# The Mamba gate turned round: D x and the gate applied with the inner dimension on partitions, and three VectorE duties moved to ScalarE and GpSimd

## The chip, the cores and the metric

The kernel runs on one core of one Trainium2 chip. A core has TensorE (PE; its weight loads are listed as PEld), VectorE (DVE), ScalarE (ACT), GpSimd (POOL) and SyncE (SP, which here only issues DMAs). Each engine takes its own instructions in the order in which the program lists them, and waits for the others through semaphores. The metric is the device time of one launch in microseconds (us); less is better.

## The reference, cut to what matters

x is 4 x 512 x 1024 (batch, time, channels), all in float32. The block is a Mamba mixer with adaptive layer norm, followed by a second mixer over four streams. The change concerns the first half alone:

```
h = layernorm(x) * (1 + ca) + sa                 # ca, sa: modulations of the batch row
x, z = split(h @ in_proj_w)                      # each 2048 inner channels ("d")
xc = silu(conv_b + sum_k conv_w[:, k] * x shifted by 3-k)   # 4 taps along time
dt_r, B, C = rmsnorm of the parts of xc @ x_proj_w.T        # 64, 16, 16 columns
dt = softplus(dt_r @ dt_proj_w.T + dt_bias)
per channel d and state n (16 of them), along time:
    state = exp(dt * A[d, n]) * state + dt * B[n] * xc
    ys   += C[n] * state
y = (ys + D * xc) * silu(z)
out = x + ga * (y @ out_proj_w.T)
```

The second half takes a layer norm of that, 24 logits a row, 50 Sinkhorn iterations on 4 x 4 matrices, and mixes four streams of 256 channels.

## The kernel before, in words

**Tiling.** Time is cut into 8 blocks of 256 (`TB`; two blocks make a batch row), `k` in the code. A block's 2048 inner channels are 16 chunks of 128 partitions, four chunks a quad (`q`, 4 quads a block, 32 in all, numbered `m`). So a tile `xc`, `u`, `dv` or `w` holds 128 partitions (channels) x 4 chunks x 256 times, 128x1024 in the profile.

**The scan loop.** The heart is 512 steps: 8 blocks x 4 quads x 16 states. For one state of one quad GpSimd makes `w = u * B` (`emit_w`, L917, two steps ahead), ScalarE makes `da = exp(dt * A)` into PSUM (`emit_exp`, L933, one step ahead), VectorE runs four scans along time in place in `w` (L963), TensorE transposes `w` so that time comes onto the partitions (`emit_turn`, L943, 8 transposes of 128x128 into `hq`, in the next step), and VectorE adds `hq * C` to `acc` (`emit_sum`, L952, two instructions of 128x512, in the next step: C is then one number a partition). `w` has three buffers, `hq` two, `da` two.

**What is put between.** `step` calls `tick` six times. A tick lets one VectorE filler out of `gaps` (a convolution tap, a norm's statistics: whatever yielded "v"), wakes the tasks whose time has come (`due`; a task yields how many ticks it sleeps: `LAG` 2, `TAP_LAG` 3, `ACT_LAG` 5, `POOL_LAG` 10), and lets `paced` issue some matmuls of the product queue. The queue (`products`) holds for block `k`: the x products of block k+1 and the output products of block k-1, alternating, then one z product, then more of both, `product_bc`, and z products. `paced` spreads these over the ticks by their columns plus an allowance `ASIDE` for work on the side; when the product at the head cannot go on (it yields 0: no bank, or an input not yet issued), nothing of the queue is issued until it can, and the columns owed are then made up at up to 1.3 times the rate. The main loop runs under a manual schedule: the order in which these calls are made is the order on each engine.

**Around the change.** `product_x` (L423) makes x of a chunk in a PSUM bank; ScalarE takes tap 3 and the bias out of it into `xc` (L448), VectorE adds taps 0 to 2 (L455), and after the fourth chunk ScalarE makes the sigmoid from tanh in a scratch tile `sg` (tag `tmp`, two buffers; L464, L465) and GpSimd multiplies (L467). `product_z` (L473) makes z with time on the partitions (`ht` is the stationary operand) and forms silu(z) in `sz`. `stage_dt` (L586), called in step 3 of the quad before, makes `dt` by softplus (L608, with a table load before and after it on ScalarE), `u = dt * xc` (L616), and then D x: ScalarE scales `xc` by D into scratch `xd` (L621), TensorE transposes it (L633), ScalarE copies it to `acc` (L638), which is where the 16 sums start from. `gate_quad` (L730), spawned in step 2 of the next quad, multiplies `acc` by `sz` on GpSimd (L735), transposes the product back (L749) and copies it to `y` (L756), the input of `product_out` (L656). `front` (L773) does the second layer norm and the logits of the block before.

**Buffers.** `xc` has five, freed by `stage_dt`; `row` tiles (128x1024) five; `sz` and `acc` two each.

## Time and profile before

| What | Value |
|---|---|
| median of 3 runs | 2709.85 us (2709.05 to 2709.86) |
| the profiled execution | 2702.3 us, span 2700.5 us, granted TensorE clock 0.94 |
| the scan loop in it | 154.6 to 2415.3 us, 512 steps |
| blocks of the loop, 1st to 8th | 315.8, 277.3, 278.7, 280.5, 279.3, 281.1, 276.1, 272.6 us |
| VectorE busy in the loop | 2090.8 of 2260.7 us |
| GpSimd busy in the loop | 1659.0 us |
| ScalarE busy in the loop | 1549.9 us |

The profile is one execution recorded by the hardware. Busy times are those of the instructions themselves; an instruction's listed duration overlaps the start of the next a little, so what one costs in a row of them is the distance between starts. In a group's row stand line, engine, operation, output <- inputs, shapes and count, then the summed time and the mean in ns, then the engine's idle time just before these instructions and what ended most of it. "x2048" of a float32 matmul counts two records for each matmul of the program; a transpose is one record. Steps are counted by the scans: a step runs from its first scan to the next step's.

### The profile page before, as it was taken

To read this page: it belongs to the slowest core of one execution; us is meant where nothing else is said; L and a number is where in the kernel's file an instruction comes from. 1 tells how busy PE (TensorE), PEld (TensorE's weight loads), DVE (VectorE), ACT (ScalarE), POOL (GpSimd) and SP (SyncE) were. 2 spreads that over 40 slices of the span, in tenths; PEclk is the share of its full clock that TensorE was granted. 3 is DMA by queue.
4 is the path that set the end of the run, shared out by engine and by line. 5 is a ranking of instruction groups with operands and counts; after the bars stand their busy time and mean duration, and the time that the engine had idled before them with its cause. 6 is when DMAs were issued, how large, how long until landed. Compare 5 with 4: busy or idle time off the path is not lost. (4 is left out here: it accounts for less than half of the span.)

```text
span 2700.5 us, 39703 instructions
## 1 busy us (share of the span) xinstructions
PE 2408.1 (89%) x13392; PEld 2051.6 (76%) x13392; DVE 2361.0 (87%) x4451; ACT 1716.9 (64%) x3755; POOL 1731.8 (64%) x1167
## 2 busy tenths in 40 slices
PE   8999989999999989998999899998999899885446
PEld 8887478888788878887888788887888777675435
DVE  0349898999999999999999999999999899977898
ACT  0356567666776777667776776668666856633445
POOL 0146557777976688768766786779676977931014
PEclk9979989999999999999999999999999899896769
DMA  5432523333433343234333433333333323225302
GB/s 184 152 125 94 204 75 130 113 106 121 154 117 104 116 153 121 106 114 149 125 110 114 156 118 109 118 145 125 121 106 124 130 94 117 83 74 203 153 31 110
DMA packets 74347, 331.06 MB, mean 123 GB/s; under 512 B 8496, under 2 KB 25312, under 8 KB 47456
## 3 DMA queue, kind: packets, MB, share of 16 engines
q1 hardware_dynamic: 62784, 311.56, 32.1%
q10 hardware_dynamic: 11360, 16.96, 1.7%
q8 instruction: 107, 1.75, 0.3%
q14 instruction: 96, 0.79, 0.1%
HBM read 303.14 MB, written 25.35 MB: 122 GB/s over the span
## 5 line engine op out<-in xcount | busy, mean ns | idle before, releaser
L917 POOL TENSOR_TENSOR w<-u,b 128x1024 f32<-128x1024 f32 x512 | 1209.1, 2363 | 558.2 <-PE hq L943 413.5
L933 ACT ACTIVATE da<-dv,aneg 128x256 f32<-128x256 f32 x2048 | 971.5, 477 | 616.5 <-DVE w L963 571.5
L963 DVE TENSOR_TENSOR_SCAN w<-da,w 128x256 f32<-128x256 f32 x2048 | 1263.3, 667 | 69.5 <-ACT da L933 47.6
L952 DVE SCALAR_TENSOR_TENSOR acc<-hq,ss,acc 128x512 f32<-128x512 f32 x1024 | 724.6, 735 | 78.2 <-PE hq L943 73.1
L943 PE MATMUL hq<-ident,w 128*128 128x128 f32 x4096 | 644.1, 282 | 73.1 <-DVE acc L952 53.7
L943 PEld LDWEIGHTS hq<-ident,w 128*128 128x128 f32 x4096 | 511.8, 146 | 220.7 <-issue 57.7
L487 PE MATMUL pz<-w_z,ht 128*128 128x256 f32 x2048 | 517.2, 387 | 0.0
L439 PE MATMUL pp<-ht,w_x 128*128 128x259 f32 x2048 | 511.5, 387 | 0.0
L667 PE MATMUL po<-y,w_out 128*128 128x256 f32 x2048 | 496.2, 381 | 5.4 <-ACT dv L608 5.4
L439 PEld LDWEIGHTS pp<-ht,w_x 128*128 128x128 f32 x2048 | 372.1, 193 | 46.2 <-issue 0.4
L667 PEld LDWEIGHTS po<-y,w_out 128*128 128x128 f32 x2048 | 368.6, 191 | 46.5 <-ACT dv L608 6.9
L487 PEld LDWEIGHTS pz<-w_z,ht 128*128 128x128 f32 x2048 | 369.2, 195 | 36.5 <-issue 0.3
L455 DVE SCALAR_TENSOR_TENSOR xc<-pp,cw,xc 128x256 f32<-128x256 f32 x384 | 178.4, 464 | 31.8 <-ACT xc L448 30.7
L1212 POOL TENSOR_TENSOR o<-o,x 128x1024 f32<-128x1024 f32 x16 | 37.7, 2354 | 189.1 <-ACT dg L1158 142.2
L1197 PE MATMUL oa<-h,dg 128*128 128x256 f32 x256 | 62.8, 389 | 74.9 <-ACT dg L1158 69.5
L1197 PEld LDWEIGHTS oa<-h,dg 128*128 128x128 f32 x256 | 49.3, 195 | 84.1 <-ACT dg L1158 76.5
L467 POOL TENSOR_TENSOR xc<-xc,sx 128x1024 f32<-128x1024 f32 x32 | 75.5, 2358 | 42.8 <-ACT sx L465 42.8
L448 ACT ACTIVATE xc<-pp,cb,cw 128x256 f32<-128x256 f32 x128 | 71.3, 557 | 47.5 <-PE pp L439 47.4
L749 PE MATMUL py<-ident,acc 128*128 128x128 f32 x256 | 48.4, 324 | 54.7 <-ACT dv L608 28.3
L262 PEld LDWEIGHTS pm<-sc,w_mod 128*128 128x128 f32 x384 | 80.9, 323 | 9.0 <-DVE mv_a L358 9.0
L262 PE MATMUL pm<-sc,w_mod 128*128 128x4 f32 x384 | 79.5, 343 | 9.1 <-DMA w_mod<-wmod_dram 9.1
L749 PEld LDWEIGHTS py<-ident,acc 128*128 128x128 f32 x256 | 34.8, 167 | 67.2 <-ACT dv L608 25.2
(172 smaller groups left out, 2303.2 us busy)
## 6 DMA issues: line engine op xcount, KB each, us to landing
w_x<-in_w_dram SPq DMA_DIRECT2D x64, 1024.0 KB, 4.7
w_z<-in_w_dram SPq DMA_DIRECT2D x64, 1024.0 KB, 4.9
w_out<-out_w_dram SPq DMA_DIRECT2D x56, 1024.0 KB, 4.8
w_mod<-wmod_dram SPq DMA_DIRECT2D x24, 1024.0 KB, 4.8
b<-bcd SPq DMA_DIRECT2D x32, 512.0 KB, 3.8
xt<-x_dram SPq DMA_DIRECT2D x16, 512.0 KB, 8.2
xr<-x_dram SPq DMA_DIRECT2D x32, 256.0 KB, 5.1
x<-xr ACTq DMA_DIRECT2D x32, 256.0 KB, 2.5
```

The source lines that it names most:

```text
L262: pe.matmul(pm[:, 2 * q + j, :], w[:, k, j * P : (j + 1) * P], sc[:, k, :], start=(k == 0), stop=(k == HC - 1),)
L439: pe.matmul(pp, w[:, h, j * P : (j + 1) * P], hts[k][:, h, :], start=(h == 0), stop=(h == HC - 1),)
L455: vec.scalar_tensor_tensor(xc[:, c, :], pp[:, tap : tap + TB], cw[:, i, tap : tap + 1], xc[:, c, :], ALU.mult, ALU.add,)
L487: pe.matmul(pz[:, t, :], hts[k][:, h, PAD + t * P : PAD + (t + 1) * P], w[:, h, :], start=(h == 0), stop=(h == HC - 1),)
L667: pe.matmul(po, w[:, d - lo, :], ys[k, d // QC][:, d % QC, :], start=(d == lo), stop=(d == hi - 1),)
L749: pe.transpose(py[:, j, t * P : (t + 1) * P], acc[:, t, c * P : (c + 1) * P], ident)
L917: pool.tensor_tensor(w, us[k, q], bts[k, n // NG][:, n % NG, :].unsqueeze(1).to_broadcast([P, QC, TB]), ALU.mult,)
L933: act.activation(da[:, j, :], dts[k, q][:, 2 * s + j, :], AF.Exp, scale=aneg[:, i, n : n + 1])
L943: pe.transpose(h[:, c * P : (c + 1) * P], ws[g][:, c, t * P : (t + 1) * P], ident)
L952: vec.scalar_tensor_tensor(acc[:, t, :], hqs.pop((g, t)), cts[k][:, t, n : n + 1], acc[:, t, :], ALU.mult, ALU.add,)
L963: vec.tensor_tensor_scan(w[:, c, :], das[g, c // 2][:, c % 2, :], w[:, c, :], 0.0, ALU.mult, ALU.add)
L1197: pe.matmul(oa[:, n, :], dg[:, n, m, :], hs[m] if m < NS else ybs[i], start=(m == 0), stop=(m == NS),)
```

## The change

Seven things are edited together.

- `product_z` swaps the operands: the weights are stationary and z comes out with channels on the partitions. `sz` has the layout of `xc`.
- `gate_quad` no longer multiplies ahead of the transposes. It transposes `acc` (now the sum over states alone), copies it to `y`, has ScalarE scale `xc` by D into a scratch tile, has GpSimd add it to `y`, and ten ticks later multiply `y` by `sz`.
- `stage_dt` therefore loses the D x scaling, its 8 transposes and the two copies.
- The first state's sum (`n == 0`) is a scaled copy on ScalarE from `hq` to `acc`, since `acc` has no starting value any more.
- `product_x` lets ScalarE scale a second tap (tap 2) into a scratch tile `sx`, taken when the quad's first x product begins; VectorE adds two taps in place of three; GpSimd adds `sx` to `xc`, and ten ticks later the sigmoid begins in `sx`.
- `xc` tiles live until the gate has read them ("xd" in place of "dt" as the mark), with six buffers in place of five; `row` tiles have four in place of five. A `sz` tile is free when `y` is done, not when the transposes are issued.
- `ASIDE` goes down by 2048, the columns of a block's 32 transposes.

```diff
@@ -111,7 +111,7 @@
 
 
 
-        free = {"mm": 4, "tmp": 2, "row": 5, "xr": 2, "ao": 2, "sgz": 1}
+        free = {"mm": 4, "tmp": 2, "row": 4, "xr": 2, "ao": 2, "sgz": 1}
         done = set()
         gaps = deque()
         waiting = deque()
...
@@ -427,10 +428,12 @@
             w = weights.pop(("x", k, p))
             m = NQ * k + q
             if p % 2 == 0:
-                if m >= 5:
-                    yield from until(("dt", m - 5), 0)
-                xcs[k, q] = quad_tile(f"xc_{k}_{q}", "xc", 5)
-            xc = xcs[k, q]
+                if m >= 6:
+                    yield from until(("xd", m - 6), 0)
+                xcs[k, q] = quad_tile(f"xc_{k}_{q}", "xc", 6)
+                yield from take("tmp", 0)
+                sxs[k, q] = scratch(f"sx_{k}_{q}")
+            xc, sx = xcs[k, q], sxs[k, q]
             for j in range(2):
                 i = 2 * p + j
                 yield from take("mm", 0)
...
@@ -449,8 +452,12 @@
                         xc[:, c, :], pp[:, PAD:], AF.Identity,
                         bias=cb[:, i : i + 1], scale=cw[:, i, KC - 1 : KC],
                     )
+                    act.activation(
+                        sx[:, c, :], pp[:, PAD - 1 : PAD - 1 + TB], AF.Copy,
+                        scale=cw[:, i, KC - 2 : KC - 1],
+                    )
                     yield TAP_LAG
-                    for tap in range(KC - 1):
+                    for tap in range(KC - 2):
                         yield "v"
                         vec.scalar_tensor_tensor(
                             xc[:, c, :], pp[:, tap : tap + TB], cw[:, i, tap : tap + 1],
...
@@ -459,12 +466,12 @@
                     give("mm")
                     if c == QC - 1:
                         yield LAG
-                        yield from take("tmp")
-                        sg = scratch(f"sx_{k}_{q}")
-                        act.activation(sg, xc, AF.Tanh, scale=0.5)
-                        act.activation(sg, sg, AF.Copy, scale=0.5, bias=0.5)
+                        pool.tensor_tensor(xc, xc, sx, ALU.add)
+                        yield POOL_LAG
+                        act.activation(sx, xc, AF.Tanh, scale=0.5)
+                        act.activation(sx, sx, AF.Copy, scale=0.5, bias=0.5)
                         yield ACT_LAG
-                        pool.tensor_tensor(xc, xc, sg, ALU.mult)
+                        pool.tensor_tensor(xc, xc, sx, ALU.mult)
                         give("tmp")
                         done.add(("xc", k, q))
 
...
@@ -476,16 +483,16 @@
                 yield from until(("h", k), 0)
                 m = NQ * k + q
                 if m >= 2:
-                    yield from until(("gate", m - 2), 0)
-                szs[k, q] = p1.tile([P, TT, 2, 2 * P], F32, name=f"sz_{k}_{q}", tag="sz", bufs=2)
-            sz = szs[k, q]
+                    yield from until(("y",) + divmod(m - 2, NQ), 0)
+                szs[k, q] = quad_tile(f"sz_{k}_{q}", "sz", 2)
+            sz = szs[k, q][:, 2 * s : 2 * s + 2, :]
             yield from take("mm", 0)
             w = weights.pop(("z", k, q, s))
-            pz = bank(f"pz_{k}_{q}_{s}", (P, TT, 2 * P))
-            for t in range(TT):
+            pz = bank(f"pz_{k}_{q}_{s}", (P, 2, TB))
+            for j in range(2):
                 for h in range(HC):
                     pe.matmul(
-                        pz[:, t, :], hts[k][:, h, PAD + t * P : PAD + (t + 1) * P], w[:, h, :],
+                        pz[:, j, :], w[:, h, j * P : (j + 1) * P], hts[k][:, h, PAD:],
                         start=(h == 0), stop=(h == HC - 1),
                     )
                     yield TB
...
@@ -495,13 +502,13 @@
             def finish():
                 yield LAG
                 yield from take("sgz")
-                sg = p1.tile([P, TT, 2 * P], F32, name=f"sgz_{k}_{q}_{s}", tag="sgz")
+                sg = p1.tile([P, 2, TB], F32, name=f"sgz_{k}_{q}_{s}", tag="sgz")
                 act.activation(sg, pz, AF.Tanh, scale=0.5)
-                act.copy(sz[:, :, s, :], pz)
+                act.copy(sz, pz)
                 give("mm")
                 act.activation(sg, sg, AF.Copy, scale=0.5, bias=0.5)
                 yield ACT_LAG
-                pool.tensor_tensor(sz[:, :, s, :], sz[:, :, s, :], sg, ALU.mult)
+                pool.tensor_tensor(sz, sz, sg, ALU.mult)
                 give("sgz")
                 if s == 1:
                     done.add(("sz", k, q))
...
@@ -614,30 +621,7 @@
             u = quad_tile(f"u_{k}_{q}", "u", 2)
             us[k, q] = u
             pool.tensor_tensor(u, dv, xc, ALU.mult)
-            yield from take("tmp")
-            xd = scratch(f"xd_{k}_{q}")
-            for c in range(QC):
-                i = QC * q + c
-                act.activation(xd[:, c, :], xc[:, c, :], AF.Copy, scale=dpar[:, i : i + 1])
-                if c % 2:
-                    yield LAG
             yield LAG
-            if NQ * k + q >= 2:
-                yield from until(("gate", NQ * k + q - 2))
-            acc = p1.tile([P, TT, QC * P], F32, name=f"acc_{k}_{q}", tag="acc", bufs=2)
-            accs[k, q] = acc
-            for t in range(TT):
-                yield from take("mm")
-                pa = bank(f"pa_{k}_{q}_{t}", (P, QC * P))
-                for c in range(QC):
-                    pe.transpose(
-                        pa[:, c * P : (c + 1) * P], xd[:, c, t * P : (t + 1) * P], ident
-                    )
-                aside(QC * TURN)
-                yield LAG
-                act.copy(acc[:, t, :], pa)
-                give("mm")
-            give("tmp")
             if k % NH:
 
                 e0 = p2.tile([P, N, QC], F32, name=f"e0_{k}_{q}", tag="e0")
...
@@ -731,11 +715,6 @@
 
             m = NQ * k + q
             acc = accs[k, q]
-            yield from until(("sz", k, q))
-            pool.tensor_tensor(
-                acc, acc, szs[k, q].rearrange("p t s c -> p t (s c)"), ALU.mult
-            )
-            yield POOL_LAG
             if m >= 6:
                 yield from until(("out", (m - 6) // NQ))
             y = quad_tile(f"y_{k}_{q}", "y", 6)
...
@@ -755,6 +734,20 @@
                 yield LAG
                 act.copy(y[:, 2 * s : 2 * s + 2, :], py)
                 give("mm")
+            yield from take("tmp")
+            xd = scratch(f"xd_{k}_{q}")
+            for c in range(QC):
+                i = QC * q + c
+                act.activation(xd[:, c, :], xcs[k, q][:, c, :], AF.Copy, scale=dpar[:, i : i + 1])
+                if c % 2:
+                    yield LAG
+            done.add(("xd", m))
+            yield LAG
+            pool.tensor_tensor(y, y, xd, ALU.add)
+            give("tmp")
+            yield POOL_LAG
+            yield from until(("sz", k, q))
+            pool.tensor_tensor(y, y, szs[k, q], ALU.mult)
             done.add(("y", k, q))
 
 
...
@@ -856,7 +849,7 @@
         XC, ZC, OC = 2 * HC * TB, 4 * HC * TB, DC * TB
         BC = 2 * DC * P
         SPLIT = DC - QC
-        ASIDE = 12416
+        ASIDE = 10368
 
         def products(k):
 
...
@@ -948,6 +941,17 @@
 
             if g >= 0:
                 k, q, n = where(g)
+                if n == 0:
+                    m = NQ * k + q
+                    if t == 0:
+                        assert m < 2 or ("gate", m - 2) in done
+                        accs[k, q] = p1.tile(
+                            [P, TT, QC * P], F32, name=f"acc_{k}_{q}", tag="acc", bufs=2
+                        )
+                    act.activation(
+                        accs[k, q][:, t, :], hqs.pop((g, t)), AF.Copy, scale=cts[k][:, t, 0:1]
+                    )
+                    return
                 acc = accs[k, q]
                 vec.scalar_tensor_tensor(
                     acc[:, t, :], hqs.pop((g, t)), cts[k][:, t, n : n + 1], acc[:, t, :],
...
```

The same two buffer counts (`row` 4, `xc` 6) also stand where such tiles are made for the modulation rows and the partial output products.

More of the change, by code (lines that the diff above doesn't have):

```diff
@@ L229, in row_tile @@
         def row_tile(name):
-            return p1.tile([P, H], F32, name=name, tag="row", bufs=5)
+            return p1.tile([P, H], F32, name=name, tag="row", bufs=4)
         def bank(name, shape):
@@ L301, in finish @@
                 yield from take("row")
-                mr = p1.tile([B, 3, TB], F32, name=f"mr_{kind}_{q}", tag="row", bufs=5)
+                mr = p1.tile([B, 3, TB], F32, name=f"mr_{kind}_{q}", tag="row", bufs=4)
                 m, sg, ab = mr[:, 0, :], mr[:, 1, :], mr[:, 2, :]
@@ L341, in load_constants @@
             vec.tensor_scalar(aneg, aneg, -1.0, None, ALU.mult)
-        hts, xcs, bts, cts, ets, szs, dts, us, accs, ys, aos, parts, e0s = ({} for _ in range(13))
+        hts, xcs, sxs, bts, cts, ets, szs, dts = ({} for _ in range(8))
+        us, accs, ys, aos, parts, e0s = ({} for _ in range(6))
         def normalize(xts, name):
@@ L681, in finish_part @@
                 if i % QC == 0:
-                    parts[i // QC] = quad_tile(f"part_{i // QC}", "xc", 5)
+                    parts[i // QC] = quad_tile(f"part_{i // QC}", "xc", 6)
                 act.activation(parts[i // QC][:, i % QC, :], po, AF.Copy, scale=scale)
```

## The prediction

> **What bounds the kernel now.** I read the page's busy shares first, then stretches of the scan loop (154.6 to 2415.3 us, 512 steps in eight blocks of 64), then the groups by line, then the order of time inside single steps. One middle block (columns: PE, PEld, DVE, ACT, POOL busy, granted clock, DMA share, GB/s):
>
> ```profile
> PE 2408.1 (89%) x13392; PEld 2051.6 (76%) x13392; DVE 2361.0 (87%) x4451; ACT 1716.9 (64%) x3755; POOL 1731.8 (64%) x1167
> ```
>
> ```profile
> 1026.40:1306.90 280.50, 264.48 (x1528) 227.91 (x1527) 263.19 (x455) 194.91 (x395) 218.45 (x177) 0.98 0.34 124
> ```
>
> VectorE works 263 of 280 us and bounds the block, but TensorE shows 264. VectorE's 17 idle us are the room for "faster for free"; TensorE's and GpSimd's limits lie close behind. The groups that the change touches:
>
> ```profile
> L963 DVE TENSOR_TENSOR_SCAN w<-da,w 128x256 f32<-128x256 f32 x2048 | 1263.3, 667 | 69.5 <-ACT da L933 47.6 <-POOL w L917 15.0 <-POOL w L922 5.1
> L952 DVE SCALAR_TENSOR_TENSOR acc<-hq,ss,acc 128x512 f32<-128x512 f32 x1024 | 724.6, 735 | 78.2 <-PE hq L943 73.1
> ...
> L455 DVE SCALAR_TENSOR_TENSOR xc<-pp,cw,xc 128x256 f32<-128x256 f32 x384 | 178.4, 464 | 31.8 <-ACT xc L448 30.7
> ...
> L735 POOL TENSOR_TENSOR acc<-acc,sz 128x1024 f32<-128x1024 f32 x32 | 75.5, 2359 | 13.2 <-DVE acc L952 13.1
> ...
> L621 ACT ACTIVATE xd<-xc,dpar 128x256 f32<-128x256 f32 x128 | 57.3, 495 | 0.0
> ...
> L700 ACT ACTIVATE ao<-po,mod_t 128x256 f32<-128x256 f32 x56 | 25.6, 458 | 1.6 <-PE po L667 1.6
> ```
>
> Means overlap with the next instruction, so I price by spacing of starts. In the order of time, VectorE's and TensorE's instructions beside each other (start, us, what):
>
> ```profile
> 1000.42 2.42 DVE L963 TENSOR_TENSOR_SCAN w<-da,w 128x256 f32<-128x256 f32 x4
> 1002.76 1.47 DVE L952 SCALAR_TENSOR_TENSOR acc<-hq,ss,acc 128x512 f32<-128x512 f32 x2
> 1004.14 2.42 DVE L963 TENSOR_TENSOR_SCAN w<-da,w 128x256 f32<-128x256 f32 x4
> ```
>
> ```profile
> 1003.71 1.03 PE L487 MATMUL pz<-w_z,ht 128*128 128x256 f32 x4
> 1004.58 0.60 PE L400 MATMUL pt<-ident,xt 128*128 128x128 f32 x4
> 1005.01 0.60 PE L487 MATMUL pz<-w_z,ht 128*128 128x256 f32 x2
> ```
>
> Four scans take 2.34 (1000.42 to 1002.76). A step of scans and sums alone, 3.64 us where nothing waits, leaves 1.30 for two sums; a tap fills 0.39 (822.66 to 823.05). Four records of 256 columns take 0.87 (1003.71 to 1004.58), and a program matmul is two of them: 0.433; four transposes take 0.43 (1004.58 to 1005.01). So a step has 0.87 us of transposes plus, at the usual six to seven matmuls, some 3.9 us of TensorE against 3.64 to 4.8 of VectorE.
>
> The reader should also see what happens where TensorE's work comes in a bunch. Near the loop's end the output products stand in six steps:
>
> ```profile
> 2375.08 2.42 DVE L963 TENSOR_TENSOR_SCAN w<-da,w 128x256 f32<-128x256 f32 x4
> 2380.05 0.75 DVE L952 SCALAR_TENSOR_TENSOR acc<-hq,ss,acc 128x512 f32<-128x512 f32 x1 [2.55 <-PE hq L943]
> ...
> 2387.87 0.24 DVE L829 SCALAR_TENSOR_TENSOR lg<-plg,r,base 128x24 f32<-128x24 f32 x1 [3.43 <-PE plg L820]
> ```
>
> The sum cannot start, because its transposes stand behind the bunch on TensorE.
>
> **The change, part by part.** Counts are from the instruction order of both built programs.
>
> VectorE loses 64 sums (1024 to 960) and 128 taps (384 to 256). In the loop that is 64 x 0.65 = 41.6 and, since the first block's 16 taps come before the loop, 112 x 0.39 = 43.7: together -85.3 us if nothing takes their place.
>
> TensorE loses 256 transposes of D x (256 x 0.108 = 27.7 us). The gate product is turned round at the same count and 387 ns a record: nothing.
>
> ScalarE gains 128 reads of a tap from PSUM. None exists; the nearest row is L700 (458 ns, scaled, from PSUM), the ends L621 (495) and L448 (557); spaced, 0.46: 59 us. The first state's scaled read takes the place of the copy of D x (585 ns, same shape): nothing. The D x scaling only moves, from after the softplus to directly ahead of it.
>
> GpSimd gains 64 additions of 128x1024 (2.36 us, the price of L735): +151 us. Its load in this block goes from 218 to some 235 of 280, so on average it fits. SP's queue has the same number of rows, and no DMA is added; a weight lands in 4.7 us and is loaded three products ahead, so its moves cost nothing unless a whole product's lead (3.5 us or more) is lost. One row buffer fewer: 0 to 8.2 us (an xt landing) a block; I take 0, since a front's rows are not needed before the next block's bunch.
>
> The new waits are in the order. The old gate multiplied first and then transposed; now a quad's output exists only after transposes, copy, D x, addition and multiplication. Behind it stand the last block's output products on TensorE. And xc exists only after an extra GpSimd addition with ten ticks' delay: behind it stands the B/C product. Third, the sixth quad's buffer is freed by the D x read and needs a scratch buffer that is now held through the whole convolution: behind it stand the x products. The planner leaves TensorE nearly empty there and pays the debt back at once. A step of an engine runs from its first instruction for that step (TensorE: the step's first transposes) to the next one's, and its load is counts times the spacings above. From the order, in us: steps 1 to 4 of the fourth block now hold 1.30, 2.17, 1.73, 0.87 of TensorE work, steps 5 to 9 hold 5.20, 6.96, 8.00, 6.06, 5.67, where VectorE has 3.64, 3.64, 3.64, 5.01, 4.03. Before, the bunch was 5.20 and 6.10 in two steps. There are two more now: steps 35 and 36 (6.12, 5.66) and 45 and 46 (6.51, 6.14).
>
> To price a bunch I carry a lag: each step adds TensorE's work less VectorE's, never below zero. What exceeds 1.30 + 2.34 - 0.87 = 2.8 us (sums and scans during which the transposes may still come) is a VectorE wait. Test: in the last 16 steps of before this gives 12.9 us; VectorE idled 14.0 there. ScalarE likewise: the exponentials of a half must come within two scans and two sums less their own length, 1.17 + 1.30 - 0.92 = 1.55. At a softplus ScalarE now has, in steps 18 and 19, 4.74 + 8.42 us (before 3.84 + 6.97), because D x and the copies stand there too. When one wait is paid, the other lag shrinks by as much.
>
> Over the loop the rule gives 102 us of waits before (TensorE 39, ScalarE 64) and 222 after (107 and 115): +119; by block before 27, 9, 11, 10, 11, 10, 9, 18 and after 32, 22, 28, 27, 28, 27, 30, 29. With wider allowances (4.2 and 2.8) it gives 61 and 159: +98. I take the middle, +108. The rule is short of the truth: VectorE idled 170 us in the loop of before, some 38 of them in the start of the first block.
>
> Outside the loop: B/C of the first block waits for the last xc (TensorE waited 6.3 us for it), which is one addition later: +2.4. At the end, the old 2.43 us multiplication before the transposes goes, and four D x (1.8) and two operations (4.7) follow the copy: +4.1, all on the path.
>
> Sum: -85.3 + 108 + 2.4 + 4.1 = +29. The profiled execution took 2702.3 us (span 2700.5), so 2732; it lies 7.5 us under the median of the runs shown, 2709.85, and on that scale the forecast is 2740.
>
> A rule that disagrees: the Trainium skill, "Perfetto Trace Analysis", section "Identifying the Most-Contended Engine", says to judge TensorE's headroom by its weight-load busy share and to relieve the busiest engine first. By that row, 228 of 280 us, TensorE has a fifth to spare and its bunches would cost nothing, which is the first rival's time. The waits of 2.55 and 3.43 us above speak against an average of either kind.
>
> **The rivals.** First, TensorE's bunches are free: ScalarE's waits of the same steps cover them, or the lag spreads. Then the 68 us of added TensorE waits go from +119: -85.3 + 51 + 6.5 = -28, 2682 on the median's scale. For it: GpSimd and ScalarE delays near step 3 give TensorE time. Against: the 14.0 us measured at the loop's end. It decides as soon as TensorE's added waits are below some 40 us.
>
> Second, the rule under-counts the new waits as it does the old ones (170 against 102, times 1.66), with GpSimd's queue as the third engine: two additions and two multiplications fall into single steps (7.56 us in step 5), and the next w, which scan and transposes need, stands behind them. 108 x 1.66 = 179: +101, 2811. Against: much of the missing 68 us is the loop's start.
>
> Third, gain and waits cancel within 0.2% (what a measurement tells from no change, 5.4 us): waits of 73 to 84 us. Nothing favours that exactly.
>
> That the change does not do what it says is excluded by the counts.
>
> **How the numbers follow.** Forecast 0.52, first rival 0.20, second 0.20, third 0.08. The forecast's own ends are its two allowances, +19 and +40: 2729 to 2750. The range reaches below the first rival and most of the way to the second: 2678 to 2798. Slower is forecast and second rival, 0.72; faster 0.20; same 0.08.
>
> **What would show it.** Right: VectorE's busy time in the loop 85 us lower; its waits for the transposes well over 100 us against 73; waits in steps 6 to 10 of blocks 2 to 7; a middle block of 280 to 288 us. Wrong: a middle block under 275, waits for transposes unchanged (first rival), or waits of the scans for GpSimd's w far above 15 us (second).

## The result, and the profile after

The changed kernel takes 2755.16 us (median of 4 runs, 2753.11 to 2763.7) against 2709.85: 1.0171 times the time before, with a 95% interval of 1.0155 to 1.0187. The ratio makes it 46.3 us slower; the two medians alone differ by 45.3. Its profiled execution took 2763.7 us (span 2761.9), the slowest of the four, and the profiled execution of before lay 7.5 us under its median, so a comparison of the two traces shows 61 us: the start is 2.3 us longer (the first scan at 156.9 against 154.6), the loop 61.5 us (156.9 to 2479.9, the end of the last scan; before 154.6 to 2416.0, since the 2415.3 given above is the start of its last scan), and the end 2.5 us shorter.

First the page's line of busy times, then a middle block in the view by stretches (length, then busy time of PE, PEld, DVE, ACT and POOL, granted clock, DMA share, GB/s), then the groups that the change touches.

```profile
PE 2427.7 (88%) x13136; PEld 2051.0 (74%) x13136; DVE 2286.5 (83%) x4259; ACT 1763.9 (64%) x3883; POOL 1875.7 (68%) x1231
```

```profile
1044.30:1330.40 286.10, 263.71 (x1493) 225.02 (x1491) 252.60 (x430) 200.65 (x410) 235.74 (x185) 0.98 0.34 121
```

```profile
L967 DVE TENSOR_TENSOR_SCAN w<-da,w 128x256 f32<-128x256 f32 x2048 | 1257.2, 668 | 122.8 <-ACT da L926 91.7
...
L956 DVE SCALAR_TENSOR_TENSOR acc<-hq,ss,acc 128x512 f32<-128x512 f32 x960 | 679.7, 736 | 159.7 <-PE hq L936 156.3
L936 PE MATMUL hq<-ident,w 128*128 128x128 f32 x4096 | 660.0, 289 | 168.7 <-DVE acc L956 115.5
...
L651 PE MATMUL po<-y,w_out 128*128 128x256 f32 x2048 | 505.4, 388 | 22.3 <-POOL y L750 22.3
...
L462 DVE SCALAR_TENSOR_TENSOR xc<-pp,cw,xc 128x256 f32<-128x256 f32 x256 | 119.3, 466 | 46.5 <-ACT sx L455 45.8
```

VectorE did lose its work: 252.60 us in this block against 263.19. The block became 5.6 us longer all the same, because VectorE now idles 33.5 us in it and idled 17.3. In the groups, its waits for the transposes rose from 73.1 to 156.3 us, those of the scans for `da` from 47.6 to 91.7. Over the loop VectorE is busy 70.9 us less and idle 132.4 us more.

Where in a block? This table is worked out from the starts of the scans in the traces: us taken by groups of four steps, mean of blocks 2 to 7. The last column is the mean block.

| steps | 0-3 | 4-7 | 8-11 | 12-15 | 16-19 | 20-23 | 32-35 | 36-39 | 44-47 | block |
|---|---|---|---|---|---|---|---|---|---|---|
| before | 17.8 | 19.4 | 16.8 | 16.9 | 17.4 | 18.2 | 17.3 | 18.2 | 17.5 | 278.8 |
| after | 17.3 | 21.4 | 23.9 | 15.4 | 17.3 | 19.3 | 16.7 | 20.6 | 18.8 | 285.9 |

Many groups gain a little; the loss is 7.1 us in steps 8 to 11, 2.0 in steps 4 to 7, 2.4 in steps 36 to 39, 1.3 in steps 44 to 47. Counted step by step in the same blocks, VectorE's idle time in steps 6 to 10, where the prediction looked for the new waits, rose from 1.9 to 10.0 us a block. The first three groups of the fifth block after, by stretches (columns as above):

```profile
1330.44:1348.41 17.97, 13.90 (x60) 10.02 (x58) 15.11 (x28) 15.36 (x37) 13.41 (x8) 0.75 0.29 110
1348.41:1369.77 21.36, 16.50 (x89) 13.88 (x89) 14.86 (x26) 13.20 (x30) 19.27 (x11) 0.97 0.21 75
1369.77:1394.37 24.60, 24.60 (x152) 22.03 (x151) 18.59 (x34) 14.16 (x31) 13.03 (x8) 1.00 0.38 129
```

TensorE gets 60 instructions in the first four steps (110 before), then 152 in steps 8 to 11 (97 before), and there it is busy without a gap while VectorE works 18.59 of 24.60 us. The order of time shows how it comes to that, first TensorE, then VectorE (start, us, what, and in brackets the idle time ahead with what ended it):

```profile
1352.68 4.48 PE L651 MATMUL po<-y,w_out 128*128 128x256 f32 x20
...
1358.30 0.60 PE L936 MATMUL hq<-ident,w 128*128 128x128 f32 x4
1361.81 1.13 PE L651 MATMUL po<-y,w_out 128*128 128x256 f32 x4 [2.90 <-POOL y L750]
...
1367.14 0.60 PE L936 MATMUL hq<-ident,w 128*128 128x128 f32 x4
```

```profile
1360.82 2.42 DVE L967 TENSOR_TENSOR_SCAN w<-da,w 128x256 f32<-128x256 f32 x4
1367.78 0.75 DVE L956 SCALAR_TENSOR_TENSOR acc<-hq,ss,acc 128x512 f32<-128x512 f32 x1 [4.54 <-PE hq L936]
```

TensorE waits 2.90 us for the last multiplication that makes `y`, then works off output and x products, and the next transposes of a state stand behind them until 1367.14. VectorE has finished its scans at 1363.24 and stands still for 4.54 us.

### The profile page after: what moved, and what is told of

Its sections match the earlier page's. It is cut to its first block, busy times and chain, and to the rows that moved or that the text cites. A ratio compares the mean times of both kernels' runs of the same rounds, so it can differ in the third digit from the quotient of the medians.

```text
span 2761.9 us, 39302 instructions
## 1 busy us (share of the span) xinstructions
PE 2427.7 (88%) x13136; PEld 2051.0 (74%) x13136; DVE 2286.5 (83%) x4259; ACT 1763.9 (64%) x3883; POOL 1875.7 (68%) x1231
## 5 line engine op out<-in xcount | busy, mean ns | idle before, releaser
L967 DVE TENSOR_TENSOR_SCAN w<-da,w 128x256 f32<-128x256 f32 x2048 | 1257.2, 668 | 122.8 <-ACT da L926 91.7
L956 DVE SCALAR_TENSOR_TENSOR acc<-hq,ss,acc 128x512 f32<-128x512 f32 x960 | 679.7, 736 | 159.7 <-PE hq L936 156.3
L936 PE MATMUL hq<-ident,w 128*128 128x128 f32 x4096 | 660.0, 289 | 168.7 <-DVE acc L956 115.5
L651 PE MATMUL po<-y,w_out 128*128 128x256 f32 x2048 | 505.4, 388 | 22.3 <-POOL y L750 22.3
L494 PE MATMUL pz<-ht,w_z 128*128 128x256 f32 x2048 | 508.7, 386 | 0.0
L442 PE MATMUL pp<-ht,w_x 128*128 128x259 f32 x2048 | 501.5, 385 | 0.0
L651 PEld LDWEIGHTS po<-y,w_out 128*128 128x128 f32 x2048 | 379.1, 195 | 67.7 <-POOL y L750 24.3
L494 PEld LDWEIGHTS pz<-ht,w_z 128*128 128x128 f32 x2048 | 371.1, 194 | 41.7 <-issue 1.3
L462 DVE SCALAR_TENSOR_TENSOR xc<-pp,cw,xc 128x256 f32<-128x256 f32 x256 | 119.3, 466 | 46.5 <-ACT sx L455 45.8
L604 PE MATMUL pd<-et,dtw 64*128 64x256 f32 x256 | 88.0, 475 | 6.3 <-ACT et L577 4.5
L451 ACT ACTIVATE xc<-pp,cb,cw 128x256 f32<-128x256 f32 x128 | 70.9, 554 | 35.1 <-PE pp L442 35.1
L469 POOL TENSOR_TENSOR xc<-xc,sx 128x1024 f32<-128x1024 f32 x32 | 75.5, 2359 | 25.9 <-DVE xc L462 25.9
L511 POOL TENSOR_TENSOR sz<-sz,sgz 128x512 f32<-128x512 f32 x64 | 81.6, 1275 | 6.1 <-ACT sgz L509 5.7
```

Of the source, the lines that this page charges most:

```text
L442: pe.matmul(pp, w[:, h, j * P : (j + 1) * P], hts[k][:, h, :], start=(h == 0), stop=(h == HC - 1),)
L462: vec.scalar_tensor_tensor(xc[:, c, :], pp[:, tap : tap + TB], cw[:, i, tap : tap + 1], xc[:, c, :], ALU.mult, ALU.add,)
L494: pe.matmul(pz[:, j, :], w[:, h, j * P : (j + 1) * P], hts[k][:, h, PAD:], start=(h == 0), stop=(h == HC - 1),)
L604: pe.matmul(pd[:, j, :], dtw[:, (QC * q + c) * P : (QC * q + c + 1) * P], ets[k][:R, :], start=True, stop=True,)
L651: pe.matmul(po, w[:, d - lo, :], ys[k, d // QC][:, d % QC, :], start=(d == lo), stop=(d == hi - 1),)
L936: pe.transpose(h[:, c * P : (c + 1) * P], ws[g][:, c, t * P : (t + 1) * P], ident)
```

## The experiments

The theory to test: the loss is one of order. `y` is issued later, the product queue finds its head not ready, and TensorE's work comes in a bunch in front of the transposes. The rivals: the 151 us of additions on GpSimd cost time of themselves; ScalarE's added or moved work does; or the first state's sum is worse off on ScalarE. The table gives every kernel that ran as a ratio to the kernel before on the same chip. "Against before" is that ratio in us of 2709.85, and differences between kernels below are differences in this column, so that runs on different chips can be set beside each other.

| kernel | median us | ratio (95% interval) | against before, us |
|---|---|---|---|
| after | 2755.16 | 1.0171 (1.0155 to 1.0187) | +46.3 |
| e1: after, queue's head changed | 2713.76 | 1.0020 (1.0011 to 1.0030) | +5.4 |
| e2: before, `y` marked ten ticks late | 2745.28 | 1.0135 (1.0119 to 1.0150) | +36.6 |
| e3: gate part alone | 2786.83 | 1.0288 (1.0260 to 1.0317) | +78.0 |
| e4: convolution part alone | 2683.41 | 0.9908 (0.9893 to 0.9923) | -24.9 |
| e5: after without GpSimd's additions | 2712.16 | 1.0018 (1.0007 to 1.0029) | +4.9 |
| e6: after without ScalarE's D scaling | 2748.97 | 1.0150 (1.0125 to 1.0176) | +40.6 |
| e7: e4, queue's head, shorter delay | 2661.79 | 0.9825 (0.9811 to 0.9840) | -47.4 |
| e8: e1 without the gate's delay | 2716.58 | 1.0027 (1.0017 to 1.0036) | +7.3 |
| e9: after, additions behind the chain | 2775.63 | 1.0234 (1.0209 to 1.0259) | +63.4 |
| e10: after, first sum on VectorE | 2738.96 | 1.0106 (1.0084 to 1.0128) | +28.7 |
| e11: e8 with a shorter delay before tanh | 2747.98 | 1.0142 (1.0121 to 1.0164) | +38.5 |
| e12: before, queue's head changed | 2684.97 | 0.9904 (0.9888 to 0.9921) | -26.0 |

### e1: another head of the product queue

The queue of a block begins with two x products instead of one, so an output product that waits for `y` comes later. Every instruction stays; only their order changes.

```diff
+                add_x(k + 1, 0, 1)
                 for i in range(4):
-                    add_x(k + 1, i, i + 1)
+                    if i < 3:
+                        add_x(k + 1, i + 1, i + 2)
                     if k:
```

> The changed kernel with one reordering of its product queue: a block begins with two x products, and each output product of the block before comes one x product later. No instruction is added or removed. Theory (the change's waits come from products that find their input not yet issued, so that TensorE stands empty and then works in a bunch): the empty steps 1 to 4 of a block hold 4.37, 4.36, 2.61, 0.87 us of TensorE work in place of 1.30, 2.17, 1.73, 0.87 and steps 7 and 8 3.94 and 4.94 in place of 8.00 and 6.06; the lag rule takes off 32 us, so about 2723 us, with VectorE's waits for the transposes some 44 us under the changed kernel's 156. Rival (the added work of ScalarE and GpSimd is what costs, wherever TensorE's work stands): as the changed kernel, 2755 us within 6.

Measured: 40.9 us less than after. The same twelve steps of the fifth block, by stretches, and VectorE's two waits:

```profile
1308.33:1325.38 17.05, 17.03 (x94) 13.76 (x93) 15.80 (x30) 13.80 (x35) 14.31 (x8) 1.00 0.35 136
1325.38:1346.51 21.13, 17.68 (x92) 15.12 (x91) 15.72 (x27) 15.99 (x32) 21.05 (x12) 0.92 0.36 125
1346.51:1363.71 17.20, 17.20 (x116) 15.64 (x115) 16.66 (x30) 12.90 (x32) 13.39 (x8) 1.00 0.26 93
```

```profile
DVE acc L958 <- PE hq L938: 100.7, 98, 8.0
DVE w L969 <- ACT da L928: 98.1, 62, 5.3
```

TensorE has 94 instructions in the first four steps, and steps 8 to 11 take 17.20 us instead of 24.60. The waits for the transposes fall from 156.3 to 100.7 us, those for `da` do not (98.1 against 91.7). The bunch costs time, and it comes from the order. Steps 4 to 7 stay at 21.13 us: GpSimd is busy there for 21.05 of them, but that this is what holds them was not tested in this order.

### e2: only the delay, in the kernel before

```diff
                 give("mm")
+            yield 10
             done.add(("y", k, q))
```

> The kernel before, with one line more: a quad's output y is marked as there 10 ticks (1.7 steps) later. No instruction is added, removed or changed; only the queue's products that ask for y are issued later. Theory: the same empty steps and bunch as in the changed kernel, at the start of each block and at the loop's end; the lag rule adds 30 us, so 2740 us, and the waits for the transposes rise from 73 to some 105 us. Rival (added work costs, not the order): 2710 us, no change.

Measured: +36.6 us. By stretches, steps 4 to 7 and 8 to 11 of its fifth block, and the wait:

```profile
1345.18:1366.53 21.35, 16.14 (x78) 13.42 (x76) 15.04 (x25) 15.80 (x35) 9.94 (x5) 0.76 0.02 3
1366.53:1389.02 22.49, 22.49 (x123) 19.74 (x122) 18.19 (x32) 11.89 (x26) 12.14 (x6) 1.00 0.42 154
```

```profile
DVE acc L953 <- PE hq L944: 117.6, 130, 8.2
```

No instruction was added to or taken from an engine, and the picture of after appears: an emptier TensorE, then 22.49 us of 22.49. Together with e1 this shows the forecast's mechanism from both sides.

### e12: the same head in the kernel before

The edit of e1, made in the kernel before.

> The kernel before with the reordered queue head alone. Theory: the bunch of steps 4 and 5 (5.20 and 6.10 us) is shared out; the rule takes off 9 us: 2700 us, 2692 to 2706. It tells how much of the best kernel's 48 us is the order and how much the convolution's part. Rival (the old order cost nothing): 2709 us within 3.

Measured: -26.0 us, more than the 10 expected. So e1's 40.9 us cannot all be put down to the change; the queue's order was worth 26.0 without it. But it acts elsewhere there: steps 8 to 11 stay (16.9 against 16.8), and steps 16 to 23 go from 35.6 to 32.0. The 6.9 us that e1 takes from steps 8 to 11 of each middle block are the change's own. Set against each other, e1 at +5.4 and e12 at -26.0 leave 31.4 us that the change still costs when both kernels have the better head; a late `y` at the block's start is thus not its whole price.

### e3 and e4: one part alone

e3 is after with the convolution of before; e4 is before with the convolution of after (a second tap on ScalarE, its addition on GpSimd, gate untouched). The core of e4's edit:

```diff
+                    act.activation(
+                        sx[:, c, :], pp[:, PAD - 1 : PAD - 1 + TB], AF.Copy,
+                        scale=cw[:, i, KC - 2 : KC - 1],
+                    )
                     yield TAP_LAG
-                    for tap in range(KC - 1):
+                    for tap in range(KC - 2):
...
+                        pool.tensor_tensor(xc, xc, sx, ALU.add)
+                        yield POOL_LAG
```

> The changed kernel with its convolution put back (three taps on VectorE, no second tap on ScalarE, no addition to xc on GpSimd); the turned gate and the first state's sum on ScalarE stay. VectorE saves 41.6 us alone. Theory: the bunch at the block's start stays, those at the sixth quad's buffer and at the B/C product go; the lag rule gives 85 us of added waits, so 2709.85 - 41.6 + 85 + 4 = 2757 us. Rival (added work): half of GpSimd's 151 us and none of ScalarE's 59 us are left, so at most half of the loss of 45 us: 2733 us or less.

> The kernel before with the convolution's part of the change alone: the second tap on ScalarE, its addition on GpSimd, two taps on VectorE. VectorE saves 43.7 us. Theory: no delayed gate, so no bunch at the block's start; a small one remains at the B/C product and ScalarE's waits grow; the lag rule adds 40 us of waits, so 2709.85 - 44 + 40 + 2 = 2708 us, between 2690 and 2720. Rival (added work): half of GpSimd's and all of ScalarE's added work is here, so half of the loss or more: 2732 us or above.

Measured: the gate part alone +78.0 us, the convolution part alone -24.9. Their sum, +53, is near the whole change's +46. The rival that puts the loss down to added work wherever it stands asked for 2733 us or less of e3 and 2732 or more of e4, and both came out the other way. The lag rule missed too: e3 is some 30 us slower than the 2757 expected, e4 some 23 us faster than the 2708, outside its range. VectorE's waits, first of e3, then of e4:

```profile
DVE acc L950 <- PE hq L930: 157.2, 146, 7.9
DVE w L961 <- ACT da L920: 77.0, 52, 4.6
```

```profile
DVE acc L958 <- PE hq L949: 89.9, 102, 7.8
DVE w L969 <- ACT da L939: 62.3, 50, 2.8
```

The gate part alone has transposes' waits as long as those of after (157.2 against 156.3); with the convolution part alone they are 16.8 us longer than before. The convolution part raises ScalarE's busy time by 43 us and GpSimd's by 72, lowers VectorE's by 51 (2310.0 against 2361.0 on the pages), and half of that arrives as time.

The Trainium skill, "Perfetto Trace Analysis", section "Optimizing Scalar/DVE Operations", says that offloading a saturated VectorE to ScalarE or even GpSimd may make sense, but that GpSimd and VectorE share a port, so that moves between these two might not help. e4 agrees with the first half. On the second the traces are split. What was moved here shows no sign of it: GpSimd's addition to `y` took 2360 ns after, the multiplication of the same shape by which it was priced 2359 before, and VectorE's scans, which read `da` from PSUM, took 665 ns (median) while GpSimd worked and 664 while it did not. But a multiplication of the second half whose operands both lie in SBUF (`sk<-sk,sa`, 128x224) took 0.39 us in the 45 cases after in which GpSimd was idle, and 1.47 us (median) in the five in which it was at work.

### e5: without GpSimd's two additions

```diff
-                        pool.tensor_tensor(xc, xc, sx, ALU.add)
                         yield POOL_LAG
...
-            pool.tensor_tensor(y, y, xd, ALU.add)
             give("tmp")
```

> The changed kernel without its two GpSimd additions (y + D x, and xc + the second tap); everything else, the delays between the calls too, stays, so all other engines have the same order. It leaves out D x and one convolution tap. GpSimd loses 64 x 2.36 = 151 us of work, all that the change added to it. Theory (order on TensorE and ScalarE): the lag rule, which GpSimd is not part of, gives no change; what goes is the shorter chain at the loop's start and end (2.4 + 2.4 us) and a part of the 22 us in which the output products waited for the gate's last multiplication (7 x 2.36 = 16 at most): 2735 to 2755 us. Rival (GpSimd's queue holds up w and with it scans and transposes): most of the loss of 45 us goes: 2720 us or less.

Measured: 41.5 us less than after, with the same order on every other engine. That is a miss for the prediction's "on average it fits" and for this run's own theory of 2735 to 2755 us; its rival's 2720 or less came true. By the scans, the bunch of steps 8 to 11 stays (23.9 us); the mean block goes from 285.9 to 281.2, the first from 322.8 to 311.7, the last from 284.8 to 275.1. TensorE's waits for `y` fall from 22.3 to 5.2 us, VectorE's for the transposes from 156.3 to 130.4.

### e9: the additions behind the chain

If GpSimd's additions cost only because `y` and `xc` wait for them, then additions of about that load that nobody waits for, just behind the two multiplications, should cost little.

```diff
-                        pool.tensor_tensor(xc, xc, sx, ALU.add)
                         yield POOL_LAG
...
                         pool.tensor_tensor(xc, xc, sx, ALU.mult)
+                        pool.tensor_tensor(sx, sx, sx, ALU.add)
...
             pool.tensor_tensor(y, y, szs[k, q], ALU.mult)
+            pool.tensor_tensor(szs[k, q], szs[k, q], szs[k, q], ALU.add)
```

> The changed kernel with GpSimd's two additions replaced by additions of the same size on scratch data, each put just behind the multiplication that it stood ahead of. It leaves out D x and one tap. GpSimd has the same 151 us of added work, but y and xc are finished one addition (2.36 us) earlier. Theory, amended after the run without additions (2712 us): what costs is that the gate's y and the convolution's xc come later to TensorE, which waits for y at a block's start with transposes standing behind; then nearly all of the 43 us goes here too: 2706 to 2725 us, and TensorE's waits for y fall from 22 us to under 8. Rival (GpSimd's load as such: w comes late because the queue is full): 2745 us or more, with VectorE's waits for w well above the changed kernel's 25 us.

Measured: 17.1 us more than after, 58.5 more than e5, although these additions of a tile to itself take 1.89 us each in place of 2.36, 121 us in all in place of 151. The waits of e9, then the last of them after:

```profile
DVE acc L956 <- PE hq L936: 157.6, 154, 8.9
...
DVE w L967 <- ACT da L926: 111.2, 47, 5.3
ACT e L635 <- POOL e L630: 72.3, 15, 6.9
```

```profile
ACT e L635 <- POOL e L630: 48.5, 16, 5.3
```

TensorE's waits for `y` fell as the theory asked, from 22.3 to 8.1 us, and the time rose all the same. So the chain alone is not the cause. Nor is it mainly what the rival named, a late `w`: the scans' waits for it are 32.6 us against 24.7. ScalarE's wait for GpSimd's `e` (a small product that `stage_dt` makes in every second block) is 33.4 us in e5, 48.5 after and 72.3 in e9, and the scans' wait for `da` goes 85.6, 91.7, 111.2. The likely reading is that what stands behind the additions in GpSimd's own queue is late, and behind it the exponentials and scans. (In the kernel before, the wait for `e` is 1.5, so the larger part comes with the gate's new order and not with the additions.) GpSimd's instructions at the start of after's fifth block show how little room there is (start, us, what):

```profile
1350.15 2.37 POOL L746 TENSOR_TENSOR y<-y,xd 128x1024 f32<-128x1024 f32 x1
1352.46 2.35 POOL L785 TENSOR_TENSOR hh<-hh,mrow 128x1024 f32<-128x1024 f32 x1
1354.78 4.67 POOL L910 TENSOR_TENSOR w<-u,b 128x1024 f32<-128x1024 f32 x2
1359.41 2.34 POOL L750 TENSOR_TENSOR y<-y,sz 128x1024 f32<-128x1024 f32 x1
1361.72 2.35 POOL L623 TENSOR_TENSOR u<-dv,xc 128x1024 f32<-128x1024 f32 x1
1364.03 2.35 POOL L910 TENSOR_TENSOR w<-u,b 128x1024 f32<-128x1024 f32 x1
```

These seven operations leave no gap in 16.2 us: a sum of D x, a multiplication by the gate, the second norm of the block before and the next quad's `u` surround the `w` that the scans need every 3.6 to 4.8 us. One reservation: in e9 the tiles `sx` and `sz` are also held for one operation more. And in the first block e9 is at 315.9 us, between e5 (311.7) and after (322.8), so there the place in the chain does count. How the 41.5 us divide between the two is open.

### e6: without ScalarE's D scaling

```diff
-                i = QC * q + c
-                act.activation(xd[:, c, :], xcs[k, q][:, c, :], AF.Copy, scale=dpar[:, i : i + 1])
...
-            pool.tensor_tensor(y, y, xd, ALU.add)
+            pool.tensor_tensor(y, y, xcs[k, q], ALU.add)
```

> The changed kernel without ScalarE's scaling by D: GpSimd adds xc itself to y, with the same delays. It leaves out the factor D. ScalarE loses 128 x 0.45 = 57 us, which stood directly ahead of the softplus. Theory, with ScalarE's lag as the second term: the rule takes off 38 us (its ScalarE part 115 to 76, TensorE's unchanged), so about 2717 us, and the scans' waits for the exponentials fall from 92 to some 55 us. Rival (TensorE's bunches alone; ScalarE's lag is hidden behind them): 2745 us or more, with the scans' waits down but those for the transposes up.

Measured: 5.7 us less than after, a difference that the two intervals do not tell from none, where the prediction's rule for ScalarE asked for 38. The mean block's steps 8 to 11 are unchanged (23.9), and the scans' waits for `da` fall only from 91.7 to 81.0 us. ScalarE's D scaling ahead of the softplus is not what makes after slow.

### e10: the first state's sum back on VectorE

```diff
-                    act.activation(
-                        accs[k, q][:, t, :], hqs.pop((g, t)), AF.Copy, scale=cts[k][:, t, 0:1]
+                    vec.tensor_scalar(
+                        accs[k, q][:, t, :], hqs.pop((g, t)), cts[k][:, t, 0:1], None, ALU.mult
                     )
```

> The changed kernel with the first state's sum put back on VectorE (a multiplication from PSUM to acc, 128x512), everything else as changed. VectorE has 64 x 0.65 = 41.6 us more, ScalarE 64 x 0.57 = 36 less. Theory (the move saved VectorE's time, and its waits came elsewhere): the rule takes off 30 us of waits, so it ends 12 us slower: 2767 us, 2755 to 2780. Rival (the move itself costs: TensorE's banks wait for ScalarE to read them, 40 us of TensorE's waits in the changed kernel): faster than the changed kernel, 2745 us or less.

Measured: 17.6 us less than after, as the rival had it, although VectorE has 64 operations more. From the waits of after and then of e10:

```profile
DVE acc L956 <- PE hq L936: 156.3, 156, 8.9
...
PE hq L936 <- ACT acc L951: 39.8, 20, 3.4
```

```profile
DVE acc L956 <- PE hq L936: 107.6, 120, 6.2
```

After, TensorE waits 39.8 us for ScalarE to read a first state out of its bank; with that read on VectorE it waits 21.7 us for it there. VectorE's waits for the transposes fall by 48.7 us ahead of the other sums, and 8.3 us of such waits stand ahead of the 64 moved ones: 40.4 less, against 32.6 us of added busy time (2319.1 against 2286.5 on the pages). The move of these sums took work off VectorE and lost time. That the late bank is the reason is not shown: TensorE's waits for VectorE's later reads rose by 13.6 us (115.5 to 129.1) at the same time, and ScalarE also had 35 us less to do.

### e8 and e11: shorter delays in the chain

e8 is e1 without the ten ticks between the gate's addition and its multiplication; e11 is e8 with five ticks instead of ten between GpSimd's addition and the tanh.

```diff
             give("tmp")
-            yield POOL_LAG
             yield from until(("sz", k, q))
```

```diff
                         pool.tensor_tensor(xc, xc, sx, ALU.add)
-                        yield POOL_LAG
+                        yield ACT_LAG
```

> The changed kernel with the reordered queue head and without the ten ticks between the gate's addition and its multiplication (both are GpSimd's, which takes them in order anyway), so that y is marked as there 1.7 steps earlier. Same instructions. Theory: the bunches at the block's start and at the loop's end shrink; the rule takes off 22 us against the reordered head alone, so about 2692 us, with waits for the transposes some 22 us lower. Rival (TensorE then waits for the multiplication itself in place of the order): 2705 us or more, with TensorE's waits for y above 22 us.

> The changed kernel with three changes of order and none of work: the queue begins with two x products, the gate has no delay between addition and multiplication, and the tanh is issued 5 ticks after the addition to xc in place of 10. Theory (order): the rule takes off 20 us against the same without the last one (2717 us), so about 2697 us; it stays above the best kernel so far (the convolution's part alone with the same order, 2662 us), since y is still late at a block's start. Rival (the delay of the tanh is hidden where the gate is late as well): 2710 us or more.

Measured: e8 1.9 us more than e1, no gain; e11 31.2 us more than e8. Both expectations of a gain fell. e11's waits:

```profile
DVE w L968 <- ACT da L927: 114.4, 70, 5.5
...
ACT sx L471 <- POOL xc L469: 47.5, 23, 4.9
```

With the earlier tanh ScalarE stands 47.5 us in its own queue waiting for GpSimd's addition (21.8 in e8), with exponentials behind it, and the scans wait 114.4 us for them (84.5). In e8 the gate's multiplication is issued earlier, and TensorE's waits for `y` fell from 20.5 to 12.6 us, the scans' for `da` from 98.1 to 84.5; but VectorE's waits for the transposes rose from 100.7 to 108.3 us, and the time did not fall. Why was not settled.

### e7: the part that pays, with the better order

e4 with e1's head of the queue and the five ticks of e11 before the tanh.

> The kernel before with the convolution's part of the change, the queue that begins with two x products, and 5 ticks in place of 10 between GpSimd's addition to xc and the tanh (ScalarE waits for the addition by itself; the delay only orders it). Theory: VectorE's saving of 43.7 us as in the convolution alone, and a smaller bunch at the block's start and before the B/C product; the rule gives 46 us less than the convolution alone, of which the head 21 and the delay 25, so about 2640 us; at least the head's part must show, 2662 us. Rival (what is left of the waits is ScalarE's softplus and does not hang on the order): 2675 us or more.

Measured: 2661.79 us, 1.75% less than before (1.60 to 1.89), and the fastest kernel of all. Its waits:

```profile
DVE acc L960 <- PE hq L951: 73.0, 81, 8.3
...
DVE w L971 <- ACT da L941: 40.0, 37, 3.2
```

The expectation of 2640 us was missed, its lower bar of 2662 met. Against e12 it is 21.4 us faster, about what e4 gains over before (24.9): the two edits nearly add up. The shorter delay was expected to gain 25 us more, of which nothing is seen; but ScalarE waits 18.5 us for `xc` here, not the 47.5 of e11. No run shows the shorter delay alone in this kernel.

## Why the prediction was right, and where its terms were not

**Direction and mechanism.** The forecast was +30 us and a slower kernel; it came out at +46 on the median's scale. Its mechanism, a late `y` that stops the product queue and bunches TensorE's work in steps 5 to 9, is shown: e2 makes the bunch by a delay alone for 36.6 us, and e1 takes it away, with 6.9 us in steps 8 to 11 of each middle block and 40.9 us in all. It is not the whole cause, since the same edit gains 26.0 us in the kernel before, elsewhere in the block, and GpSimd's additions cost 41.5 us with the bunch in place.

**VectorE's -85.3 us.** Nearly right in a middle block: -10.6 there, where 8 sums and 16 taps make -11.4. Over the loop only -70.9. Of the missing 14.4 us some 6 are in the last block, which should have lost 8 sums and is busy 247.0 us against 245.8, because more of the second half's operations fall into it and some of them last longer beside GpSimd. The rest is spread over the other blocks.

**The added waits, +108.** VectorE idles 132.4 us more in the loop. The rule's split was near: +68 for TensorE against 83 measured at the transposes, +51 for ScalarE against 44 at `da`. GpSimd's `w` grew by 9.7 us (15.0 to 24.7). Of the forecast's signs, the waits for the transposes and those in steps 6 to 10 were met, and the middle block, at 285.9 us, lay inside 280 to 288; the busy time that VectorE should lose was not. The prediction's own waits before, block by block, add to 105 us and not to its 102, which changes nothing in the forecast.

**GpSimd, "on average it fits", priced at nothing.** This is the term that failed most. e5 measures 41.5 us for it. A load of 235 of 280 us does not tell that an operation of 2.36 us finds room where it stands.

**ScalarE's first sum, "nothing", and its -41.6 us on VectorE.** e10 shows the gain given back and 17.6 us more. What was missing is what the moved read does to others; that TensorE gets its bank back later, 39.8 us of its waits, is a part of it whose price is open.

**ScalarE's D scaling.** Put directly ahead of the softplus, it was held to be a wait; e6 measures 5.7 us. So the total was nearer than its terms, and that was luck: without GpSimd's additions, and so without the 4.7 us that two of them add at the start and the end, the same order on the other engines costs +4.9 us and not some +25, and the missing GpSimd price made up for it. As a price the lag rule did no better in the experiments. What it expected against before, and what was measured: e2 +30 and +36.6, e1 +13 and +5.4, e12 -10 and -26.0, e3 +47 and +78.0, e4 -2 and -24.9, e10 +57 and +28.7, e8 -18 and +7.3, e11 -13 and +38.5. It named the places; it did not tell what removing one wait leaves of the others. The waits of the trace overlap, so a wait's length at an engine is no price for removing its cause.

**Start and end.** +2.3 us at the start (forecast +2.4). The wait in question, which the prediction put at 6.3 us, is 4.48 us in the first block before and 6.55 after; 6.3 was the sum of five such waits of the whole run. At the end -2.5 (forecast +4.1). The traces show why in part: from the end of the last scan to the last output products it now takes 11.5 us in place of 8.6, so the longer chain is there with +2.9, and what follows is 5.4 us shorter, which no run looked into.

**The rivals.** The first, that TensorE's bunches are free, is refuted by e1 and e2; with it the reading that a weight-load share of 228 of 280 us leaves TensorE a fifth to spare. In steps 8 to 11 TensorE was busy for all of 24.60 us with weight loads in 22.03, so a share of nine tenths was already the end of its room. The second, GpSimd's queue as a third engine, was right in kind and too high in size: 41.5 of the +46 go with it, but the waits of VectorE that name GpSimd's `w` rose by only some 10 us; the longer waits of ScalarE for `e` and of TensorE for `y` suggest that most of it arrives through these two.

## What to carry to other kernels

When engines take their work in order, look at what a move puts ahead of what, step by step, on every engine and not only on the busiest, and look for stretches where one of them is busy all the time right after a stretch with far fewer instructions (152 after 60 and 89 here). Split a change before judging it: here one part gained 25 us and the other lost 78. A delay alone, added to the kernel before, is a cheap way to test whether an order can be the cause. And an edit that mends the changed kernel should be tried in the kernel before as well: here it gained 26.0 us there, in other steps.

## What the runs showed that was not expected

The granted clock fell where the order left TensorE little to do. In the first four steps of after's fifth block it was 0.75, in e1's 1.00. Two TensorE lines of after, then one of e1 (start, us, what) show the same dt product at two speeds:

```profile
1339.07 1.69 PE L936 MATMUL hq<-ident,w 128*128 128x128 f32 x8 [2.97 <-ACT acc L951]
...
1341.54 2.07 PE L604 MATMUL pd<-et,dtw 64*128 64x256 f32 x4
```

```profile
1321.31 1.13 PE L604 MATMUL pd<-et,dtw 64*128 64x256 f32 x4
```

After an idle time of 2.97 us the product takes 2.07 us instead of 1.13, and the granted clock from 1341 to 1347 us is 0.50. The idle time alone does not decide it: after the 2.90 us ahead of 1361.81 the clock stayed at 1.00. The Trainium skill, "TensorE: Matmul & The Clock Gate", section "Part 1: The HAM clock gate", says that the array falls to half its clock after an idle window of about 3.4 us; the rows agree in kind, with half the clock, a factor of 1.83 in the product's time and a gap somewhat below that window. The clock did not make the main loss: these four steps took 17.97 us against 17.77, and the bunch in steps 8 to 11 ran at 1.00. What the slow dt products add in steps 4 to 7 was not measured apart.

The other surprise is e12: the kernel before had 26.0 us to gain from the order of its queue alone.
